# Turning later band groups ahead of their run, inside the feed-forward steps

## The chip, the cores and the metric

The kernel runs on one core of one Trainium2 chip. The metric is device time in microseconds, the median of three runs. A core has five engines that run side by side and wait for each other through semaphores: PE (matrix products; the profile shows its weight loads apart, as PEld), DVE (vector work), ACT (functions of single elements), POOL (a second engine for vector work) and SP, which in this kernel issues nearly all transfers. Products land in eight PSUM banks; everything else is in SBUF or, for inputs, results and two kinds of intermediate data, in DRAM.

## The reference

The input x has shape (2, 256, 128, 128): batch, time, band, channel. Three layers follow, each added to x. Attention over time is causal, with 4 heads of 32; attention over bands is limited to 16 neighbours on either side; the third is a feed-forward layer with 512 hidden channels. Each begins with a normalization over the channels.

```
xt = _ln(x, ln_t_w, ln_t_b).transpose(0, 2, 1, 3)
x = x + _mha(xt, t_wi, t_bi, t_wo, t_bo, H_T, cm).transpose(0, 2, 1, 3)
xf = _ln(x, ln_f_w, ln_f_b)
x = x + _mha(xf, f_wi, f_bi, f_wo, f_bo, H_F, bm)
xn = _ln(x, ln_n_w, ln_n_b)
h = jax.nn.gelu(xn @ w1.T + b1, approximate=False)
x = x + (h @ w2.T + b2)
```

All is float32.

## The kernel before

The work is cut into 384 groups of 512 tokens (128 partitions times NT = 4 columns of 128 channels). The first 128 groups (`OverTime`) do attention over time and write to DRAM. Then come 16 runs. A run holds 8 groups of attention over bands (`OverBands`) and then the same 8 pieces of data as feed-forward groups (`FeedForward`). The input of a band group is read from DRAM; a feed-forward group takes the result of its band group from SBUF.

`BoundedPath.run` (line 1275) goes through the groups in one loop over steps n (line 1313). A step issues pieces of several groups: PE's products for group n, the second part of n - 1, the end of n - 2, and the preparation of later groups. Every instruction goes through `InOrder` (line 897), so each engine, and SP as well, does its work in exactly the order of the calls in the loop; one operation that waits keeps back all behind it on its engine. The profile therefore shows line 907 for nearly everything, and instructions are told apart by their tiles.

How a group is prepared:

- `statistics` (line 390): on DVE, four BATCH_NORM_STATS2 and four BATCH_NORM_AGGREGATE make mean and variance (tiles stats, mv). `root` (line 407): two operations on POOL make rstd, one over the deviation. Band groups get both one run ahead, in the feed-forward step 8 groups earlier (lines 1417 to 1423; those of the first band group come a step later, with the second's).
- `normalize` (line 441): on DVE, four TENSOR_SCALAR, from x to xh (2 buffers).
- `turn` (line 458): one STREAM_TRANSPOSE on DVE from xh to z (2 buffers), then four transfers issued by SP that write z to a DRAM buffer, turned. The pool of these buffers is named turns (line 928).
- `fetch` (line 470): one transfer that reads turned back as xnT, the operand of PE.

Before the change the step in which normalize and turn stand is n + 3 for every band and feed-forward group (line 1384); fetch is issued in the step for n + 2 (line 1376), ahead of it; PE uses xnT of a feed-forward group in step n itself and of a band group one step earlier.

PSUM: in these runs the eight banks go round (`turn_of_bank`, line 943). A feed-forward step takes, in this order, two banks for the first two hidden products (`first_half`, tiles xnT and w1f), one for the output of the group before (`weigh`, tiles hT and w2T_sb, called zp in the code), and two for the other two hidden products (`second_half`). ACT empties the hidden banks with Gelu. DVE empties the output bank in `divide` (line 886), an addition to res; this call stands at line 1406, behind the normalize and turn of the same step. res is then written to the output, with four transfers on SP for every second group.

In a band step DVE has these: `first_function` (line 790), which clamps and masks the scores of the fourth head (bank<-bank,band) ahead of its Exp on ACT; normalize and turn; `finish` (x<-bank,x); three operations of `divide` (line 615); and, in some steps, statistics for feed-forward groups. In the first feed-forward step (called turn in the loop) `invert_exactly` puts one RECIPROCAL in place of two functions on ACT. In the first run, DVE also tests the weights in the third and fourth feed-forward step (`test`, line 1162), and PE sums the tests in the sixth (`verdict`, line 1174).

Of the kernel before, what the change touches and what calls it, by code (L numbers as in the profile page):

```python
# [17 lines left out]
DRAM = bass.MemoryType.DRAM  # L18
# [7 lines left out]
NT = 4  # L26
# [343 lines left out]
class Group:  # L370
# [7 lines left out]
    def __init__(self, path, src, dst, before=None, store=None):  # L378
        self.path, self.src, self.dst = path, src, dst
        self.before, self.store = before, store  # L380
# [531 lines left out]
class BoundedPath:  # L912
    def __init__(self, ctx, tc, k):
        self.tc, self.nc, self.k = tc, tc.nc, k
        self.xpool = ctx.enter_context(tc.tile_pool(name="xpool", bufs=3))
        self.work = ctx.enter_context(tc.tile_pool(name="work", bufs=3))
        self.small = ctx.enter_context(tc.tile_pool(name="small", bufs=6))
        ps = ctx.enter_context(tc.tile_pool(name="ps", bufs=1, space=PSUM))
        self.ps = [ps.tile([P, BANK], F32, name=f"bank{i}", tag=f"bank{i}") for i in range(8)]
        self.next_bank = 0  # L920
        self.inputs = 0
        self.held = {}
        self.banks = dict(zip(("a1", "a2", "b0", "b3", "a0", "a3", "b1", "b2"), range(8)))
        self.tensor, self.vector = InOrder(tc, tc.nc.tensor), InOrder(tc, tc.nc.vector)
        self.scalar, self.gpsimd = InOrder(tc, tc.nc.scalar), InOrder(tc, tc.nc.gpsimd)
        self.sync = InOrder(tc, tc.nc.sync)
        k.wf, k.bq, k.wn, k.orow = [], [], [], []
        self.dram = ctx.enter_context(tc.tile_pool(name="turns", bufs=3, space=DRAM))
        self.zero = 0.0
        self.once = once = ctx.enter_context(tc.tile_pool(name="once", bufs=1))  # L930
        self.tests = once.tile([P, 6], F32, name="tests")
        self.eps = once.tile([P, 1], F32, name="eps")
        tc.nc.vector.memset(self.eps, EPS)

        self.band = once.tile([P, P], F32, name="band")
        tc.nc.gpsimd.memset(self.band, 0.0)
        for s in (1, -1):
            tc.nc.gpsimd.affine_select(
                out=self.band, in_=self.band, compare_op=ALU.is_ge, fill=-1e30, base=BAND,
                pattern=[[-s, P]], channel_multiplier=s,  # L940
            )
# [333 lines left out]
    def run(self, x, out):  # L1275
        groups = list(self.groups(x, out))

        def do(n, *names):
            if 0 <= n < len(groups):
                for name in names:  # L1280
                    getattr(groups[n], name)()

        def at(n, kind):
            return 0 <= n < len(groups) and isinstance(groups[n], kind)

        def do_at(n, kind, *names):
            if at(n, kind):
                do(n, *names)
# [6 lines left out]
        run0 = [i for i in range(len(groups)) if at(i, OverBands)][: RUN // NT]  # L1295
# [6 lines left out]
        def statistics_of_feed(n):  # L1302
            if n + 5 in early:
                do(n + 5, "statistics")
            if at(n + 4, FeedForward) and n + 4 not in early:
                do(n + 4, "statistics", "root")

        groups[-1].last = True

        ff = [i for i in range(len(groups)) if at(i, FeedForward)][2:]  # L1310
# [2 lines left out]
        for n in range(len(groups) + 2):  # L1313
            feeds = [at(n - 2 + i, FeedForward) for i in range(5)]
            bands = [at(n - 2 + i, OverBands) for i in range(5)]
            turn = feeds[2] and bands[1]
# [64 lines left out]
                k.late_weights()  # L1381
            for i in {0: (), 1: (), 2: (14, 15), 3: (16, 17)}.get(n, (n + 14,)):
                do(i, "load")
            do_at(n + 3, (OverBands, FeedForward), "normalize", "turn")
            if n != 1:
                do_at(n + 4, OverTime, "normalize", "turn")
            if old is not None:
# [125 lines left out]
```

## Time and profile before

| | us |
|---|---|
| median of 3 runs | 2633.2 |
| lowest and highest run | 2632.67, 2638.77 |
| span of the profiled execution | 2631.9 |
| time groups, from the start to about | 930 |
| one run of 8 band and 8 feed-forward steps, about | 106 |

The profiled execution gives a span of 2631.9 us, from the first to the last instruction; the granted TensorE clock was 1.000 throughout. The table of stretches cuts the span where the reader asks and sums each engine's busy time in each stretch. The timeline lists instructions in order of start, equal neighbours merged (x4 is four of them), with start, time from the first start to the last end, engine, operation and tiles, and in brackets how long the engine had idled before and what ended that. A tile name stands for all its buffers; bank stands for all eight banks, so that which bank is meant follows from the code.

### The profile page before, as it was taken

To read this page: it belongs to the slowest core of one execution; us is meant where nothing else is said; L and a number is where in the kernel's file an instruction comes from. 1 tells how busy PE (TensorE), PEld (TensorE's weight loads), DVE (VectorE), ACT (ScalarE), POOL (GpSimd) and SP (SyncE) were. 2 spreads that over 40 slices of the span, in tenths; PEclk is the share of its full clock that TensorE was granted. 3 is DMA by queue.
4 is the path that set the end of the run, shared out by engine and by line. 5 is a ranking of instruction groups with operands and counts; after the bars stand their busy time and mean duration, and the time that the engine had idled before them with its cause. 6 is when DMAs were issued, how large, how long until landed. Compare 5 with 4: busy or idle time off the path is not lost.

```text
span 2631.9 us, 156460 instructions
## 1 busy us (share of the span) xinstructions
PE 2617.8 (99%) x68688; PEld 1837.4 (70%) x68688; DVE 2140.8 (81%) x6410; ACT 1838.8 (70%) x3543; POOL 1958.6 (74%) x2311
## 2 busy tenths in 40 slices
PE   9999999999999999999999999999999999999999
PEld 6666666666766767666777776667676677777776
DVE  8888888888888887977878779788797797887974
ACT  7989988999899875564655746647557466475573
POOL 7999999999999987666667666665776666757762
PEclk9999999999999999999999999999999999999999
DMA  6656555565565454445454544554454445554543
GB/s 155 167 149 158 149 149 149 155 155 149 149 158 149 122 127 119 115 123 127 118 124 124 123 122 117 126 128 120 122 126 120 120 119 131 123 120 123 123 104 88
DMA packets 469797, 344.97 MB, mean 131 GB/s; under 512 B 43120, under 2 KB 404464, under 8 KB 469104
## 3 DMA queue, kind: packets, MB, share of 16 engines
q1 hardware_dynamic: 468408, 334.41, 50.5%
q8 instruction: 540, 8.85, 1.5%
q14 instruction: 153, 1.25, 0.2%
q10 hardware_dynamic: 696, 0.46, 0.1%
HBM read 167.98 MB, written 166.72 MB: 127 GB/s over the span
## 4 chain that ended last, share of the span: by engine, by line
PE 99%; DVE 0%; issue 0%; DMA 0%; ACT 0%; ACTq 0%; DVEq 0%
PE bank L907 99%; DMA x<-in_x 0%; DVE xh L907 0%; DVE bank L907 0%; DVE res L907 0%; DVE stats L907 0%; DVE oT L907 0%; DVE u L907 0%; DVE xnT L907 0%; ACTq L907 0%; ACT p L907 0%; DVE vy L907 0%; ACT lnv L907 0%; DVE mv L907 0%; ACT root L907 0%
## 5 line engine op out<-in xcount | busy, mean ns | idle before, releaser
L907 ACT ACTIVATE hT<-bank,b 128x512 f32<-128x512 f32 x512 | 348.1, 688 | 524.2 <-PE bank L907 483.2
L907 POOL TENSOR_SCALAR_AFFINE_SELECT pf<-pf 128x512 f32<-128x512 f32 x768 | 477.7, 637 | 185.3 <-ACT pf L907 159.1
L907 PEld LDWEIGHTS bank<-w2T_sb,hT 128*32 128x32 f32 x16384 | 467.4, 110 | 54.8 <-issue 29.0
L907 PE MATMUL bank<-xnT,wf 128*32 128x512 f32 x4096 | 492.4, 592 | 0.5 <-DVE xnT L907 0.5
L907 PE MATMUL bank<-xnT,w1f 128*32 128x512 f32 x4096 | 486.3, 592 | 0.2 <-issue 0.2
L907 PE MATMUL bank<-w2T_sb,hT 128*32 128x128 f32 x16384 | 482.8, 273 | 1.0 <-issue 1.0
L907 ACT ACTIVATE p<-bank 128x512 f32<-128x512 f32 (+1 forms) x1024 | 430.6, 494 | 62.9 <-PE bank L907 62.9
L907 DVE TENSOR_SCALAR xh<-x,mv,rstd 128x160 f32<-128x160 f32 (+1 forms) x1012 | 394.3, 432 | 59.7 <-POOL rstd L907 49.4
L907 POOL TENSOR_SCALAR_AFFINE_SELECT p<-p 128x1024 f32<-128x1024 f32 (+2 forms) x384 | 364.5, 949 | 57.5 <-ACT p L907 49.1
L907 PEld LDWEIGHTS bank<-wf,xnT 128*32 128x32 f32 x8192 | 243.3, 110 | 144.1 <-issue 101.6
L907 POOL TENSOR_TENSOR p<-p,p 128x512 f32<-128x512 f32 x256 | 324.6, 1291 | 10.6
L907 DVE BATCH_NORM_STATS2 stats<-x 128x6 f32<-128x128 f32 x1536 | 329.0, 276 | 3.4 <-DMA x<-in_x 3.4
L907 POOL TENSOR_SCALAR rstd<-mv 128x4 f32<-128x4 f32 x251 | 57.8, 230 | 361.7 <-DVE mv L907 360.5
L907 PEld LDWEIGHTS bank<-xnT,w1f 128*32 128x32 f32 x4096 | 183.6, 110 | 171.6 <-issue 109.6
L907 PE MATMUL bank<-qT,kT 32*64 32x80 f32 (+4 forms) x16384 | 302.0, 271 | 0.1
L907 PEld LDWEIGHTS bank<-qT,kT 32*64 32x64 f32 x16384 | 260.0, 131 | 51.2 <-ACT kT L907 50.6
L907 DVE TENSOR_TENSOR res<-bank,res 128x512 f32<-128x512 f32 (+1 forms) x259 | 170.3, 658 | 153.3 <-PE bank L907 144.7
L907 ACT ACTIVATE pf<-bank 128x512 f32<-128x512 f32 x512 | 265.8, 602 | 35.5 <-PE bank L907 31.3
L907 PE MATMUL bank<-wn,oT 128*32 128x128 f32 x8192 | 283.8, 274 | 0.1
L907 DVE STREAM_TRANSPOSE z<-xh 128x512 f32<-128x512 f32 x380 | 270.3, 711 | 13.3
L907 PE MATMUL bank<-wf,xnT 128*32 128x128 f32 x8192 | 276.5, 273 | 0.0
L907 POOL TENSOR_TENSOR rstd<-rstd,mhalf 128x4 f32<-128x4 f32 x251 | 260.8, 1039 | 20.9
(100 smaller groups left out, 3820.3 us busy)
## 6 DMA issues: line engine op xcount, KB each, us to landing
turned<-z SPq DMA_DIRECT2D x1520, 64.0 KB, 2.7
xnT<-turned SPq DMA_DIRECT2D x380, 256.0 KB, 3.2
x<-res SPq DMA_DIRECT2D x256, 128.0 KB, 2.5
x<-x SPq DMA_DIRECT2D x128, 256.0 KB, 4.1
out<-res SPq DMA_DIRECT2D x252, 128.0 KB, 2.3
x<-in_x SPq DMA_DIRECT2D x124, 256.0 KB, 4.3
x<-in_x SPq DMA_DIRECT2D x4, 128.0 KB, 2.8
x<-in_x SPq DMA_DIRECT2D x6, 64.0 KB, 2.9
```

The costliest lines, as they stand in the source:

```text
L907: return self.tc.keep_in_program_order(emit(*args, **kwargs))
```

## The change

The call at line 1384 is replaced by a function that looks three and six groups ahead. Three ahead it does what was done before, unless the group has been turned already. Six ahead it normalizes and turns a band group, if that group is not of the first run. All band groups of a later run are so turned in step n + 6: the first three in the third to fifth feed-forward step (before: the sixth to eighth), the 4th to 6th in the sixth to eighth feed-forward step (before: the first three band steps), the 7th and 8th in the first two band steps (before: the fourth and fifth). Feed-forward groups stay at three ahead. By steps of a run this makes one block of normalize and turn more in each of the third, fourth and fifth feed-forward steps, where it stands behind the block of a feed-forward group, and one less in each of the third, fourth and fifth band steps. In all others their number is the same. The pool of DRAM buffers for turned grows from 3 to 8.

```
-        self.dram = ctx.enter_context(tc.tile_pool(name="turns", bufs=3, space=DRAM))
+        self.dram = ctx.enter_context(tc.tile_pool(name="turns", bufs=2 * NT, space=DRAM))
...
+        def turn_ahead(n):
+            for i in (n + 3, n + 6):
+                if at(i, FeedForward) and i == n + 3 or at(i, OverBands) and (i == n + 3 or n > run0[0] and i not in run0):
+                    if not hasattr(groups[i], "turned"):
+                        do(i, "normalize", "turn")
...
-            do_at(n + 3, (OverBands, FeedForward), "normalize", "turn")
+            turn_ahead(n)
```

## The prediction

> **What bounds the kernel now.** Read first the busy shares on the page and the waits of PE in the stretch of the band and feed-forward runs (1040 to 2600 us; the columns of a wait are its total in us, how often, the longest).
>
> ```profile
> PE 2617.8 (99%) x68688; PEld 1837.4 (70%) x68688; DVE 2140.8 (81%) x6410; ACT 1838.8 (70%) x3543; POOL 1958.6 (74%) x2311
> ...
> PE bank L907 <- issue: 2.7, 7, 0.8
> ```
>
> PE is covered for 99% of the span, and of these 1560 us it waited visibly for 2.7, never for DVE. But the page says that matmul ends are modelled, so short stalls can hide under neighbours. Hence the second reading, the table of stretches, one line a step, in the fourteenth run (its feed-forward steps are called f0 to f7, the band steps b0 to b7; the band groups that f2 to f7 prepare are the next run's). Columns: stretch, its length, then PE, PEld, DVE, ACT, POOL busy.
>
> ```profile
> 2339.93:2346.16 6.23, 6.23 (x188) 4.23 (x184) 6.09 (x18) 5.08 (x10) 4.98 (x8) 1.00 0.51 118
> 2368.92:2375.85 6.93, 6.93 (x172) 5.48 (x166) 5.39 (x27) 2.05 (x4) 5.58 (x7) 1.00 0.35 97
> 2375.85:2382.78 6.93, 6.93 (x166) 5.37 (x162) 6.86 (x33) 2.75 (x5) 6.64 (x9) 1.00 0.39 88
> 2382.78:2389.71 6.93, 6.93 (x166) 5.42 (x162) 6.71 (x26) 2.75 (x5) 6.74 (x9) 1.00 0.61 156
> 2389.71:2396.64 6.93, 6.93 (x166) 5.42 (x162) 4.73 (x19) 2.76 (x5) 6.79 (x7) 1.00 0.80 208
> 2396.64:2403.57 6.93, 6.93 (x166) 5.42 (x162) 3.92 (x16) 2.75 (x5) 4.25 (x5) 1.00 0.42 102
> ```
>
> Line 1 is a band step: DVE 6.09 of 6.23 us, full. The others are f2 to f6 by the start of PE's step: DVE is full in f3 and f4 (6.86 and 6.71 of 6.93) and has room only from f5 on (4.73, then 3.92). The change puts its work into f2, f3 and f4. So the question is not how much DVE has on average but how late it already is there, and what waits for it.
>
> **Part 1, band steps: what is removed.** Three normalize-and-turn blocks per run leave steps b2, b3, b4. (Steps b0 and b1 still do one each, for the 7th and 8th group.)
>
> ```profile
> 2327.47 0.70 DVE L907 SCALAR_TENSOR_TENSOR bank<-bank,band 128x512 f32<-128x512 f32 x1 [0.63 <-PE bank L907]
> 2347.12 0.67 DVE L907 SCALAR_TENSOR_TENSOR bank<-bank,band 128x512 f32<-128x512 f32 x1
> 2352.61 0.69 DVE L907 SCALAR_TENSOR_TENSOR bank<-bank,band 128x512 f32<-128x512 f32 x1
> ...
> 2339.66 1.07 PE L907 MATMUL bank<-pf,ones 128*32 128x512 f32 x8
> 2345.89 1.22 PE L907 MATMUL bank<-pf,ones 128*32 128x512 f32 x8
> 2352.28 1.05 PE L907 MATMUL bank<-pf,ones 128*32 128x512 f32 x6
> ```
>
> The clamp of the fourth head came at once in b3 (DVE had idled 0.63). Three steps of 6.23 later it is due at 2346.16 and comes at 2347.12: in b6, DVE has fallen 0.96 us behind (the clamps of b4 and b5 by part of it). The fourth head's Exp and its row of ones-products, a step later, hang on the clamp, and there PE shows it: 2339.66 to 2345.89 is 6.23, the next step 6.39, 0.16 more. Bounds of the gain per run: nothing (the skew lost in the next block) and 0.96 (all the lag). I take what PE shows, 0.16; 15 runs (the first is not touched) make 2.4 us, at most 14.4.
>
> The entry into the feed-forward steps has a second one:
>
> ```profile
> 2367.52 0.43 DVE L907 TENSOR_SCALAR oT<-u 128x512 f32<-128x512 f32 x1
> 2366.16 0.59 PE L907 MATMUL bank<-xnT,w1f 128*32 128x512 f32 x1
> 2368.00 1.14 PE L907 MATMUL bank<-wn,oT 128*32 128x128 f32 x30
> ```
>
> The last band group's output product starts at 2368.00, 0.05 after its operand (2367.95). Two hidden products before it, from 2366.16, take 1.72 (half of the 3.44 of four, below), so it was due at 2367.88: 0.12 waited. Between nothing and 0.12 a run I take the middle, 0.06: 0.9 us in 15.
>
> **Part 2, feed-forward steps: what is added.** One block more in each of f2, f3, f4 (the 1st to 3rd band group of the next run; f5 to f7 have one before and after, of other groups).
>
> ```profile
> 2377.02 1.60 DVE L907 TENSOR_SCALAR xh<-x,mv,rstd 128x160 f32<-128x160 f32 x4
> 2378.66 0.71 DVE L907 STREAM_TRANSPOSE z<-xh 128x512 f32<-128x512 f32 x1
> 2379.30 0.83 DVE L907 BATCH_NORM_STATS2 stats<-x 128x6 f32<-128x128 f32 x4
> 2380.32 0.66 DVE L907 TENSOR_TENSOR res<-bank,res 128x512 f32<-128x512 f32 x1
> 2385.23 0.66 DVE L907 TENSOR_TENSOR res<-bank,res 128x512 f32<-128x512 f32 x1
> 2389.31 0.65 DVE L907 TENSOR_TENSOR res<-bank,res 128x512 f32<-128x512 f32 x1
> 2395.38 0.69 DVE L907 TENSOR_TENSOR res<-bank,res 128x512 f32<-128x512 f32 x1 [2.13 <-PE bank L907]
> ...
> 2381.03 0.60 PE L907 MATMUL bank<-xnT,w1f 128*32 128x512 f32 x2
> 2384.47 3.73 PE L907 MATMUL bank<-w2T_sb,hT 128*32 128x128 f32 x126
> 2387.96 0.60 PE L907 MATMUL bank<-xnT,w1f 128*32 128x512 f32 x2
> 2394.89 0.60 PE L907 MATMUL bank<-xnT,w1f 128*32 128x512 f32 x2
> ```
>
> Price of a block: from 2377.02 to the next operation at 2379.30, 2.28 us, with no idle time near it. In program order the new block stands right behind the old one and ahead of the addition res that empties the previous group's output bank. The four res rows are those of f1, f2, f3, f4. The last one waited for PE, so there DVE has caught up; the first three did not.
>
> Who waits for res? The eight banks go round. A feed-forward step takes five: hidden 0 and 1 of its group, the output of the group before, hidden 2 and 3. Eight turns after f1's output (taken in f2) come: hidden 2 and 3 of f2; hidden 0, 1, output, hidden 2, 3 of f3; hidden 0 of f4. So hidden 0 of f4 must wait until res of f1 has read the bank, and likewise f5 for f2, f6 for f3. A stretch of four hidden products runs 2381.03 to 2384.47, 3.44 us; its second half is hidden 0 and 1 of the next group, so hidden 0 of f4 starts at 2382.75, of f5 at 2389.68, of f6 at 2396.61. The ends of res are 2380.98, 2385.89, 2389.96. Slack today: 1.77, 3.79, 6.65 us. Ahead of them come one, two, three new blocks, 2.28, 4.56, 6.84. **Late by 0.51, 0.77, 0.19**: PE stands 0.51 at f4, another 0.26 at f5, and at f6 the 0.77 already lost is cover enough. DVE does not wait for PE there, so nothing of it comes back: 0.77 us a run, 14 runs, 10.8 us.
>
> In the first run DVE also has the weight tests in f2 and f3 and is later:
>
> ```profile
> 1013.40 0.65 DVE L907 TENSOR_TENSOR res<-bank,res 128x512 f32<-128x512 f32 x1
> 1016.91 0.39 PE L907 MATMUL bank<-tests,ones 128*128 128x6 f32 x2
> ```
>
> This res is f3's; the verdict's product in f5 takes the bank that hidden 0 of f6 takes elsewhere. 14.05 + 6.84 = 1020.89 against 1016.91: 4.0 us once.
>
> The block's inputs hide: its rstd must be there when DVE has done the old block, 2379.30.
>
> ```profile
> 2378.09 1.04 POOL L907 TENSOR_TENSOR rstd<-rstd,mhalf 128x4 f32<-128x4 f32 x1
> ```
>
> It ends at 2379.13, 0.17 ahead. That cover is thin: each 0.1 that POOL is later adds 0.1 to every lateness. The later blocks' rstd were made a step before. Below that, bounds of the added cost: 0 a run, if DVE had a block's room, and 2.28 a run, a whole block. The slack of 1.77 lies nearer to the block than to nothing of it, and gives the 0.5 to 0.8 taken.
>
> Queues: each added block issues four more writes of turned on SP ahead of the step's stores and of the next step's fetch.
>
> ```profile
> 2379.40 2.38 SPq L907 DMA_DIRECT2D turned<-z  x4
> 2381.83 1.99 SPq L907 DMA_DIRECT2D out<-res  x4
> 2383.99 1.21 SPq L907 DMA_DIRECT2D xnT<-turned  x1
> xnT<-turned SPq DMA_DIRECT2D x380, 256.0 KB, 3.2
> ```
>
> Four writes took 1.9 to 2.4 us. In f2 the new four run from 2381.8 to 2383.7, the stores behind them (res at 2383.26) to 2385.7, and the fetch of f5's operand starts at 2385.7 instead of 2383.99. With 3.2 to land it is there at 2388.9, ahead of 2389.68; cost nothing, with 0.8 us of cover (1.3 with the stall). The larger ring of DRAM buffers (3 to 8) costs no instruction; it is needed as up to five turned groups lie between write and fetch. ACT and PE get no instruction more or less.
>
> **Sum.** +10.8 + 4.0 - 2.4 - 0.9 = +11.5 us on the profiled span of 2631.9, which is 1.3 under the median 2633.2 (start and end around the span): 2644.7 us. Own range of this case: 2640 (0.5 us lost and 0.3 gained a run) to 2649 (0.85 lost and nothing gained).
>
> **Rivals.**
>
> A, the delay is absorbed: not slower. PE's slack for the bank is larger than the starts show, or DVE reaches f0 earlier by the 0.96 that it no longer lags and hands that on; it decides once the slack at f4 is 2.28 instead of 1.77. Against: before it reaches f0 the lag is worked off: the clamp of b7 comes at 2352.61, four steps of 6.23 after 2327.47 are 2352.39, so 0.2 can be handed on, of the 0.5 needed. Then only part 1 stays: 2633.2 - 3.3 = 2629.9. The Trainium skill, Perfetto Trace Analysis, section Identifying the Most-Contended Engine, says that matmul busy time does not tell how far PE is from its limit and that the busy share of weight loads does: by that rule PE has 30% to spare (70% above, 5.42 of 6.93 in these steps) and might win 0.8 us back. The trace disagrees: three steps in which DVE is early or late last 6.93 alike, so there is no faster pace to return to.
>
> B, SP is late too. If the fetches for f5 and f7, both behind a step's stores, land after 4.3 us instead of 3.2, as the 256 KB loads of the input do, f5's comes 0.3 us after its time, or hides in the stall; with a slow issue like the 1.21 above it is 1.2. At 0.5 us a run: 2652.
>
> ```profile
> x<-in_x SPq DMA_DIRECT2D x124, 256.0 KB, 4.3
> ```
>
> C, faster: all 0.96 us of DVE's lag was PE's, and the slack suffices. 2633.2 - 14.4 = 2618.8. Against: PE shows 0.16 of it. The Trainium skill, Perfetto Trace Analysis, section Optimization Strategy, holds that where the most loaded engine changes between stages, mixing the stages can pay; this is its case in this kernel. The table speaks against the place: the mixed-in work falls on f3 and f4, which are as full as the band step.
>
> D, nothing: blocks stay where they were, or gain and loss cancel. 2633.2. The condition on the group's index holds from the second run on, so the blocks do move.
>
> **How the numbers follow.** A measurement of this kernel tells about 0.3% from no change, 7.9 us: 2625.3 to 2641.1. Forecast 0.55 (of it 0.06 under 2641.1), A 0.21, B 0.12, C 0.06, D 0.06. Slower: 0.49 + 0.12 = 0.61; within: 0.06 + 0.21 + 0.06 = 0.33; faster: 0.06. The range goes from A, 2629, to 2651, half of B: it leaves out C and half of B, and some of A and of the forecast's edges, under 0.2.
>
> **What would show it.** Right: in the timeline of after, in every run, DVE without idle time from the last band steps to f5; the res of f1 ends after PE's hidden products of f3 are done, and hidden 0 of f4 starts right behind it; steps f4 and f5 last 7.4 and 7.2 us, not 6.93; the band steps are 6.23 throughout. Wrong: f4 and f5 at 6.93 (A); hidden 0 of f5 starting with its fetch's landing rather than with res (B); band steps shorter than 6.23, or feed-forward steps shorter than 6.93 (C). The sum falls most easily by the 0.5 us: a slack wrong by that much is the whole of it.

## The result and the profile after

| | before | after |
|---|---|---|
| median, 6 runs each | 2633.7 us | 2651.3 us |
| lowest and highest run | 2632.67, 2638.77 | 2646.08, 2657.28 |
| span of the profiled execution | 2631.9 us | 2649.7 us |

The changed kernel is slower: its ratio to before is 1.0067, with a 95% interval of 1.0054 to 1.0080, which is 17.6 us at the medians. The forecast was slower by 11.5 us, 2644.7, with an upper end of 2651.0. The sign and the main mechanism came as predicted; the time lies 0.3 us above the range and 6.6 above the forecast: one term that the sum has at zero was not zero.

The page of before has these two lines that the prediction did not show, the shares of the chain that ended last and the group of the first hidden products (busy time and mean; behind the second bar, idle time ahead of them and what ended most of it):

```profile
PE 99%; DVE 0%; issue 0%; DMA 0%; ACT 0%; ACTq 0%; DVEq 0%
L907 PE MATMUL bank<-xnT,w1f 128*32 128x512 f32 x4096 | 486.3, 592 | 0.2 <-issue 0.2
```

The page of after, with the busy shares and the median landing time of the fetches as well:

```profile
PE 2622.6 (99%) x68688; PEld 1766.7 (67%) x68688; DVE 2141.2 (81%) x6410; ACT 1836.0 (69%) x3543; POOL 1957.1 (74%) x2311
...
PE 79%; DVE 16%; DMA 2%; POOL 1%; issue 1%; SPq 1%; ACT 0%; ACTq 0%; DVEq 0%; POOLq 0%
...
L907 PE MATMUL bank<-xnT,w1f 128*32 128x512 f32 x4096 | 478.8, 593 | 15.1 <-DVE res L907 7.0
...
xnT<-turned SPq DMA_DIRECT2D x380, 256.0 KB, 3.4
```

The busy shares say nothing: PE stands at 99% in both. The chain does. It was PE alone, and now a fifth of it is DVE, transfers and SP. The hidden products, which had waited for nothing, wait 15.1 us. What for is in PE's waits from 1040 to 2620 us (total, how often, the longest):

```profile
PE bank L907 <- DVE res L907: 4.6, 13, 0.4
PE bank L907 <- DMA xnT<-turned: 4.6, 5, 1.2
PE bank L907 <- issue: 1.8, 4, 0.5
PE bank L907 <- DVE mv L907: 1.6, 2, 0.9
PE bank L907 <- DVE stats L907: 1.4, 4, 0.5
```

The first is the bank that the prediction named, once in nearly every run. The second, a fetch that has not landed, has no term in its sum. The last two have to be read with care. No hidden product uses mv or stats; a wait for several semaphores is put down to the one that came last, and these too turn out to be fetches, since they stand at f5 and f7 with the bank long free.

The stretches of the fourteenth run, by the start of PE's steps, answer to those of before (b5, then f3 to f6; columns as there):

```profile
2361.15:2367.38 6.23, 6.23 (x190) 4.14 (x184) 6.09 (x17) 5.06 (x9) 4.97 (x8) 1.00 0.50 127
2390.86:2398.32 7.46, 7.11 (x165) 4.43 (x157) 7.32 (x28) 3.12 (x6) 4.90 (x8) 1.00 0.45 102
2398.32:2405.46 7.14, 7.13 (x160) 4.43 (x160) 7.00 (x28) 2.47 (x4) 4.99 (x7) 1.00 0.71 186
2405.46:2412.41 6.95, 6.95 (x160) 4.56 (x164) 6.81 (x26) 2.67 (x4) 6.87 (x7) 1.00 0.44 102
2412.41:2419.66 7.25, 7.11 (x165) 4.44 (x158) 7.11 (x26) 2.91 (x6) 6.96 (x9) 1.00 0.78 182
```

Step f3, from the start of f3 to that of f4, takes 7.46 instead of 6.93, and f4 7.14; both were forecast (7.4 and 7.2, there called steps f4 and f5, after the steps whose start is late). f5 has 6.95. But f6 takes 7.25, which was not forecast. The granted clock is 1.00 throughout, so no step is longer by the clock.

The same spacings for all of the 14 middle runs, summed over what the step takes undisturbed, give this account of the profiled executions (each number is a sum of start-to-start distances of PE's steps):

| place | before | after | forecast of the difference |
|---|---|---|---|
| step f3 (14 runs), 6.93 each | 0.6 | 7.5 | +7.1 |
| step f4, 6.93 each | 0.0 | 6.7 | +3.6 |
| step f6, 6.93 each | 0.0 | 5.4 | 0 |
| the first run's f3 to f6 | 0.6 | 4.6 | +4.0 |
| band steps b1 to b5 (15 runs), 6.23 each | 6.0 | 3.0 | -2.4 |
| entry into the feed-forward steps (15 runs) | 2.1 | 1.2 | -0.9 |

These differences add up to 19.1 us, and the spans differ by 17.8; the rest lies outside the places listed. Step f3 takes 7.45 to 7.54 in every one of the 14 runs. Step f4 takes 7.14 to 7.30 in eight of them and 7.46 to 8.33 in the other six. In f6, seven runs have 6.93 to 6.95 and seven 7.09 to 8.36. So there is a fixed part, the bank, of 6.9 + 14 x 0.22 = 10.0 us, and a part that comes and goes, 3.6 in f4 and 5.4 in f6: 9 us.

The ninth run shows both parts in one step. PE in the timeline:

```profile
1861.70 1.92 PE L907 MATMUL bank<-xnT,w1f 128*32 128x512 f32 x16 [0.34 <-DVE res L907]
...
1870.04 1.92 PE L907 MATMUL bank<-xnT,w1f 128*32 128x512 f32 x16 [1.20 <-DMA xnT<-turned]
```

DVE there, the additions that free the two banks:

```profile
1860.99 0.66 DVE L907 TENSOR_TENSOR res<-bank,res 128x512 f32<-128x512 f32 x1
...
1868.14 0.66 DVE L907 TENSOR_TENSOR res<-bank,res 128x512 f32<-128x512 f32 x1
```

And what SP issues ahead of f5:

```profile
1857.83 5.08 SPq L907 DMA_DIRECT2D turned<-z  x8
1863.01 1.95 SPq L907 DMA_DIRECT2D out<-res  x4
1865.06 0.43 SPq L907 DMA_DIRECT2D xnT<-turned  x1
```

f4 starts 0.05 after the addition for f1 ends (1861.65), as forecast. For f5 the bank is free at 1868.80, but PE starts at 1870.04: its operand was fetched at 1865.06, behind the four stores and eight writes instead of four, and 4.98 us passed until PE could begin, not 3.2. The trace also has the landing of these fetches: those for f5 took 2.95 to 4.85 us from issue to landing in the 14 middle runs, median 3.77, and in seven of these runs PE starts f5 within 0.14 us of the landing (here it came at 1869.90). There the fetch alone ended the wait.

### The profile page after: what moved, and what is told of

It is laid out like the page before. It is cut to its first block, busy times and chain, and to the rows that moved or that the text cites. A ratio compares the mean times of both kernels' runs of the same rounds, so it can differ in the third digit from the quotient of the medians.

```text
span 2649.7 us, 156373 instructions
## 1 busy us (share of the span) xinstructions
PE 2622.6 (99%) x68688; PEld 1766.7 (67%) x68688; DVE 2141.2 (81%) x6410; ACT 1836.0 (69%) x3543; POOL 1957.1 (74%) x2311
## 4 chain that ended last, share of the span: by engine, by line
PE 79%; DVE 16%; DMA 2%; POOL 1%; issue 1%; SPq 1%; ACT 0%; ACTq 0%; DVEq 0%; POOLq 0%
PE bank L907 79%; DVE xh L907 5%; DVE stats L907 3%; DVE z L907 2%; DVE ln L907 1%; DMA xnT<-turned 1%; DVE res L907 1%; DVE mv L907 1%; POOL rstd L907 1%; SPq L907 1%; DVE x L907 1%; DMA turned<-z 1%; DVE bank L907 1%; DVE u L907 0%; DMA x<-x 0%
## 5 line engine op out<-in xcount | busy, mean ns | idle before, releaser
L907 PEld LDWEIGHTS bank<-w2T_sb,hT 128*32 128x32 f32 x16384 | 453.9, 110 | 69.8 <-issue 54.3
L907 PE MATMUL bank<-xnT,w1f 128*32 128x512 f32 x4096 | 478.8, 593 | 15.1 <-DVE res L907 7.0
L907 PE MATMUL bank<-w2T_sb,hT 128*32 128x128 f32 x16384 | 474.5, 273 | 1.6 <-issue 1.3
L907 PEld LDWEIGHTS bank<-xnT,w1f 128*32 128x32 f32 x4096 | 134.1, 110 | 230.5 <-issue 167.1
L907 PE MATMUL bank<-wn,oT 128*32 128x128 f32 x8192 | 276.3, 274 | 0.6 <-issue 0.5
L907 POOL TENSOR_TENSOR rstd<-rstd,mhalf 128x4 f32<-128x4 f32 x251 | 260.6, 1038 | 20.9
L907 DVE TENSOR_TENSOR bank<-bank,r 128x512 f32<-128x512 f32 x240 | 166.9, 695 | 102.1 <-PE bank L907 80.9
```

Of the source, the lines that this page charges most:

```text
L907: return self.tc.keep_in_program_order(emit(*args, **kwargs))
```

## The experiments

The theory from here on: **bank plus fetch**. DVE's late addition costs about 10 us and 4 in the first run, late fetches of f5 and f7 about 9, and the band steps give back 3 to 4. The rival: **one cause**, in which the fetches are late only because the bank wait shifts PE against SP, so that mending the bank mends both; and for the fetches alone, that they were a chance of one execution or only cover some other stall. All times are medians; each ratio is to the kernel before on the same chip.

| experiment | us | before there | ratio, 95% interval |
|---|---|---|---|
| e1_res_first | 2666.2 | 2631.4 | 1.0120 [1.0098, 1.0142] |
| e2_fetch_first | 2647.4 | 2631.4 | 1.0055 [1.0038, 1.0072] |
| e3_both_first | 2651.2 | 2631.4 | 1.0073 [1.0056, 1.0090] |
| e4_last_three | 2630.9 | 2631.4 | 0.9996 [0.9986, 1.0005] |
| e5_split | 2632.3 | 2631.2 | 0.9998 [0.9989, 1.0008] |
| e6_one_f2 | 2641.2 | 2631.2 | 1.0040 [1.0025, 1.0054] |
| e7_one_f3 | 2631.1 | 2631.2 | 0.9999 [0.9989, 1.0008] |
| e8_ring | 2630.9 | 2631.2 | 0.9997 [0.9987, 1.0006] |
| e9_after_again | 2651.3 | 2630.4 | 1.0077 [1.0062, 1.0093] |
| e10_fetch_first_again | 2643.6 | 2630.4 | 1.0045 [1.0032, 1.0058] |
| e11_two_writes | 2644.9 | 2630.4 | 1.0051 [1.0037, 1.0066] |

### One block at a time: e6, e7, e4

Only one of the three blocks stays early. For e6 it is the 1st band group's, in f2; for e7 the 2nd's, in f3:

```
-                if at(i, FeedForward) and i == n + 3 or at(i, OverBands) and (i == n + 3 or n > run0[0] and i not in run0):
+                place = (i - run0[0]) % (2 * RUN // NT)
+                if i == n + 3 and at(i, (FeedForward, OverBands)) or at(i, OverBands) and n > run0[0] and i not in run0 and place == 0:
```

(e7 has place == 1.)

> Only the 1st band group of a later run is turned early, in the third feed-forward step (one block more in f2, one less in f5); all others as before the change. BANK: f3 lasts 7.46 in every run (2.28 against 1.77), f4 has no bank's wait (2.28 against 3.79), only a fetch for f5 that is late at times (up to 1 us); f6 6.93. 7 us of bank, 1 to 5 of fetch, 0.6 in the first run: 2639 to 2645. If DVE's load as such were the cause, f4 and f5 would be longer too.

> Only the 2nd band group of a later run is turned early, in the fourth feed-forward step (one block more in f3, one less in f6): the same work as in the sixth experiment, one step later. BANK: res of f2 is 2.28 late against 3.79, res of f3 against 6.65: no wait, f3 and f4 6.93. The step's stores do not stand between the new writes and the fetch for f6, so no late fetch either. 2631 to 2634, and 0.6 to 1 of it in the first run. DVE LOAD: as slow as the sixth experiment, since f3 is as full as f2's neighbours.

The waits of PE in e6, from 1040 to 2620 us:

```profile
PE bank L907 <- DVE res L907: 2.0, 11, 0.2
PE bank L907 <- DMA xnT<-turned: 1.4, 3, 0.8
```

One block in f2 costs 10.0 us: step f3 is 7.2 us over in 14 runs, 0.52 a run (the prediction had 0.51), and step f4 another 3.6, most of it by late fetches (up to 7.91). The same block in f3 costs nothing: the sums over f3 to f6 are those of before. It fits into the slack of 3.79 at f5, as the single block in f2 does not fit into the 1.77 at f4. That confirms the prediction's slacks, one by one.

e4 leaves the 1st to 3rd group as before and keeps what the change does to the 4th to 8th (two blocks each in f5, f6 and f7):

```
-                if at(i, FeedForward) and i == n + 3 or at(i, OverBands) and (i == n + 3 or n > run0[0] and i not in run0):
+                later = n > run0[0] and i not in run0 and at(i - 3, OverBands)
+                if at(i, FeedForward) and i == n + 3 or at(i, OverBands) and (i == n + 3 or later):
```

> The first three band groups of a run are turned where they were before (sixth to eighth feed-forward step); the 4th to 6th, 7th and 8th as in the changed kernel. So f5, f6, f7 have two blocks each and f2, f3, f4 one; the band steps are those of the changed kernel. DVE has 4.73 and 3.92 of 6.93 us busy there, room for 2.28. BANK+FETCH: no wait for a bank or a fetch, the band's gain alone: 2627 to 2631. Rival THE MOVE ITSELF (turning six ahead costs by its longer way or more live buffers, wherever it stands): 2640 or more.

Its waits of PE:

```profile
PE bank L907 <- issue: 1.8, 6, 0.5
PE bank L907 <- ACT pf L907: 0.2, 1, 0.2
```

Steps f3 to f6 are back at 6.93, but for two of the 14 f3 steps (7.01 and 7.22; before has one of 7.48), and the band step that the prediction had at 6.39 before is 6.23, as in the changed kernel. So the gain in the band steps exists by itself, and the three blocks in f2 to f4 bring the whole loss. In time the gain is not resolved: the interval allows 3.7 us of gain and 1.3 of loss, and the forecast of 3.3 lies in it.

### Which wait is whose: e1, e2, e3, e5

e1 puts the six-ahead block behind the addition res, in every step:

```
-        def turn_ahead(n):
-            for i in (n + 3, n + 6):
+        def turn_ahead(n, ahead):
+            for i in (n + ahead,):
...
-            turn_ahead(n)
+            turn_ahead(n, 3)
...
             do(n - 1, "divide")
+            turn_ahead(n, 6)
```

> The blocks turned six ahead stand behind the addition res of their step instead of ahead of it; nothing else differs from the changed kernel. Theory BANK+FETCH (the loss is 0.53 + 0.22 us a run of waiting for the output bank, 4 in the first run, and some 0.64 us a run of late fetches for the operands of f5 and f7): the bank's part goes, since res of f1, f2, f3 is then late by no, one, two blocks of 2.28 against slacks of 1.77, 3.79, 6.65; steps f3 and f4 return to 6.93 where the fetch is in time; SP has as many writes as before, so 1 to 5 us of late fetches stay. 2634 to 2640 us. Rival FETCH ALONE (the bank's waits hide behind fetches that would be late anyway): 2647 to 2652. Rival DVE LOAD (three blocks in full steps cost PE whatever their order): 2649 to 2653.

A miss by 26 us, and of use. Its waits of PE:

```profile
PE bank L907 <- issue: 9.8, 13, 3.0
PE bank L907 <- ACT kT L907: 7.4, 14, 0.6
PE bank L907 <- DMA xnT<-turned: 5.9, 10, 1.2
```

The wait for res is gone, and step f3 is 6.93 in all 14 runs: the bank is proved. The fetches are still late (step f4 up to 9.11), which is against the rival of one cause: without any bank wait they cost more, not less. And a new wait has come, in band step b1. DVE there:

```profile
2347.82 0.70 DVE L907 TENSOR_TENSOR bank<-bank,r 128x512 f32<-128x512 f32 x1 [2.41 <-ACT r L907]
...
2349.35 0.69 DVE L907 TENSOR_TENSOR oT<-bank,u 128x512 f32<-128x512 f32 x1
2349.95 1.60 DVE L907 TENSOR_SCALAR xh<-x,mv,rstd 128x160 f32<-128x160 f32 x4
2351.59 0.71 DVE L907 STREAM_TRANSPOSE z<-xh 128x512 f32<-128x512 f32 x1
2352.23 0.67 DVE L907 SCALAR_TENSOR_TENSOR bank<-bank,band 128x512 f32<-128x512 f32 x1
2352.80 0.68 DVE L907 TENSOR_TENSOR x<-bank,x 128x512 f32<-128x512 f32 x1
2354.71 0.70 DVE L907 TENSOR_TENSOR bank<-bank,r 128x512 f32<-128x512 f32 x1 [1.23 <-ACT r L907]
```

The same place in the changed kernel:

```profile
2333.33 0.71 DVE L907 STREAM_TRANSPOSE z<-xh 128x512 f32<-128x512 f32 x1
2334.20 0.70 DVE L907 TENSOR_TENSOR bank<-bank,r 128x512 f32<-128x512 f32 x1
...
2335.72 0.69 DVE L907 TENSOR_TENSOR oT<-bank,u 128x512 f32<-128x512 f32 x1
2336.49 0.70 DVE L907 SCALAR_TENSOR_TENSOR bank<-bank,band 128x512 f32<-128x512 f32 x1
```

In the changed kernel the block ends with the transpose that starts at 2333.33, just ahead of the first operation of `divide`, and the clamp follows oT at once (2336.49). In e1 DVE idles 2.41 there, waiting for ACT's reciprocal r, and the block comes behind oT; it stands ahead of the clamp, which comes 2.9 us after oT's start instead of 0.8. ACT's Exp and the next r, which hang on the clamp, come later, and DVE idles another 1.23. So ahead of `divide` the block had filled a wait; behind it, it lengthens the next one. ACT also copies kT late, and PE takes 6.87 or more for b1 in 14 of the 15 later runs (6.23 undisturbed). Steps b2 and b3 are 14.0 us over as well, summed over these runs (1.7 before), in some of them and by up to 3.2 us, mostly without a visible cause; so the loss of e1 is not explained to the end.

e2 sends the stores of a feed-forward group behind the fetch of the next step, so that they no longer stand ahead of it (those of the last three groups stay):

```
-        self.store()
+        if self.last or self.at_once:
+            self.store()
...
             do_at(n + 2, (OverBands, FeedForward), "fetch")
+            if at(n - 2, FeedForward) and not groups[n - 2].at_once:
+                groups[n - 2].store()
```

> The four stores of a feed-forward group are issued behind the next step's fetch instead of ahead of it; DVE's order is that of the changed kernel. BANK+FETCH: the bank's waits stay (f3 7.46, f4 7.15 in every run), the fetches of f5 and f7 leave SP 2 us earlier and are in time, so f4 is never over 7.2 and f6 is 6.93 in every run: 9 us less, 2641 to 2644, and the runs lie closer together than the 2646 to 2657 of the changed kernel. FETCH ALONE: all of the loss goes, 2628 to 2634. DVE LOAD: 2649 to 2653.

In its profile step f3 stays at 7.46, f4 is 7.15 (7.24 in two runs) and f6 6.93, and no fetch is waited for. The total fell less than expected, to 3.4 us over the upper end: in that execution stalls without a visible cause ("issue", up to 1.2 us) in b1 and b2 took part of it. For that reason it was run again, below.

e3 is e1 and e2 together.

> Both reorderings at once. BANK+FETCH: no loss is left but some of the first run's, the band steps' gain of 3 to 6 us stays: 2627 to 2632, faster than before. DVE LOAD: 2649 to 2653. A third cause that neither order touches would leave it over 2635.

That is 19 us over what was expected, and over the 2635 at which the expectation had put a third cause. Step f3 is down to 6.94 and f4 to 6.98 in the mean, but f5 has 5.7 us over in 14 runs: the fetch for f6 now stands on SP behind four stores and eight writes, and goes out 3.4 us ahead of its use in the fourteenth run. b1 has its 6.87 or more again, in all 15 later runs, and b2 and b3 are 5.8 over. The new order moves the shortage to other places.

e5 turns the three blocks at the end of steps f2 to f4 and issues their writes behind the next step's fetch; the 4th to 8th group are as in the change:

```
+            if behind(n + 5):
+                do(n + 5, "send")
...
+            if behind(n + 6):
+                do(n + 6, "normalize", "flip")
```

> The 1st to 3rd band group are still normalized and transposed in the third to fifth feed-forward step, but at that step's end, behind the addition and the statistics, and their four writes of turned are issued in the next step behind its fetch; the other groups as in the changed kernel. BANK+FETCH: res of f1 is not delayed, res of f2 by 2.28 (slack 3.79), of f3 by 4.56 (slack 6.65), and no fetch stands behind a new write that waits for DVE. So f3 to f6 last 6.93 in every later run, the first run loses some 1.4 us of its 4, and the total is that of the kernel with two blocks in each of the last three steps, 2630 to 2633. Rival ORDER DOES NOT HELP (as the first and third experiment might be read, 2666 and 2651): 2645 or more, with late products in f3 to f6.

It is level with before. Steps f3 and f4 are 6.93 in 13 of the 14 runs (once 7.64 and once 7.26); some fetches for f7 are late (3.7 us over all runs). All blocks are still moved and the loss is gone: what cost the time was their place ahead of res and ahead of the fetch, not the work. No version is measurably under before; e4 and e5 only match it.

e8 is before with the ring of eight DRAM buffers and nothing else.

```
-        self.dram = ctx.enter_context(tc.tile_pool(name="turns", bufs=3, space=DRAM))
+        self.dram = ctx.enter_context(tc.tile_pool(name="turns", bufs=2 * NT, space=DRAM))
```

> The kernel before with 8 DRAM buffers for turned instead of 3, nothing else. BANK+FETCH: no difference that can be told, 2631 to 2634. Rival RING (longer way between write and read of a buffer, other addresses, costs in DMA): 2640 or more, with late fetches as in the changed kernel.

It is level, so the ring costs nothing that can be told.

### The size of the fetch: e9, e10, e11

e9 is the changed kernel and e10 is e2 again, timed side by side.

> The changed kernel once more, beside the next one, so that the fetch's part is read from one chip. Theory (the excess is a bank wait of about 10 us and late fetches of about 9 us, less some 4 us of gain): 2646 to 2653, steps f3 to f4 at 7.45 in every later run, f4 to f5 7.15 or more, f6 to f7 over 6.93 in about half of them. Rival (the late fetches of the profiled execution were an accident of it): the same f3 to f4, but f4 to f5 at 7.15 and f6 to f7 at 6.93, and about 2643.

> The changed kernel with the stores of a feed-forward group behind the next step's fetch, once more. Theory (late fetches cost about 9 us): no late fetch, f4 to f5 at 7.15 and f6 to f7 at 6.93, and 4 to 9 us under e9; the earlier run of it was some 4 us under the changed kernel's median, on another chip. Rival (late fetches only hide a stall that then shows elsewhere): within 2 us of e9.

The waits of PE in e10:

```profile
PE bank L909 <- DVE res L909: 4.3, 13, 0.4
PE bank L909 <- issue: 3.1, 6, 1.0
```

And SP around the fetch for f5 in its fourteenth run:

```profile
2392.41 0.34 SPq L909 DMA_DIRECT2D xnT<-turned  x1
2392.80 2.98 SPq L909 DMA_DIRECT2D out<-res  x4
```

The fetch now goes out 0.49 after f4's start (2391.92) and no step waits for it; from issue to use there are 5.4 to 6.8 us at f5 and 4.8 to 6.4 at f7. e10 is 7.7 us under e9, inside the 4 to 9 expected. That is the fetch in total time, and not a sharp figure: the executions of e9 lie between 2644.4 and 2658.1, those of e10 between 2640.6 and 2645.5, and e2, the same order on another chip, was 3.9 under the changed kernel's median. In the profile of e9 the late fetches take 5.2 us (1.9 in f4, 3.3 in f6), against 9 in the first profile. What is left is 13.2 us over before, with an interval of 8.4 to 15.3: the bank and the first run less the gains, for which the forecast had 11.5.

e11 asks whether SP's load alone makes the fetch late, with no block added on DVE: the kernel before with the ring of eight, and with f5 to f7's own turned data written once more to a DRAM buffer that nothing reads. These groups are turned in f2 to f4, so the copies are issued there; where the expectation speaks of the next run's band groups, and of f5 to f7 as the place, it is mistaken.

```
+        if self.twice:
+            spare = path.dram.tile([H, D, NT, P], F32, name="spare")
+            for i in range(NT):
+                path.sync.dma_start(spare[:, :, i, :].rearrange("c a x -> a c x"), z[rows_of(i)])
...
+            groups[i].twice = (i - run0[0]) % (2 * A) in (A + 5, A + 6, A + 7)
```

> The kernel before with eight DRAM buffers and, in f2, f3 and f4 of the runs 0 to 14, a second copy of the writes of the next run's 1st to 3rd band group: SP has the transfers that the change adds there, DVE none of its blocks. Here the copied group is the one that the kernel before turns, so the copies are issued in f5, f6 and f7 of each run, not earlier. Theory (a late fetch needs only four writes more ahead of it on SP): the fetches behind them are issued about 1.9 us later; those with a lead under 5 us are late at times, and 2 to 6 us over the kernel before. Rival (it needs DVE's lag as well): all steps at 6.93, and level with the kernel before, 2631.

The fifth run of e11, PE, DVE and SP in the timeline:

```profile
1435.04 1.92 PE L912 MATMUL bank<-xnT,w1f 128*32 128x512 f32 x16 [0.78 <-DVE stats L912]
```

```profile
1429.48 0.66 DVE L912 TENSOR_TENSOR res<-bank,res 128x512 f32<-128x512 f32 x1
```

```profile
1425.60 3.86 SPq L912 DMA_DIRECT2D spare<-z  x4
1429.56 1.94 SPq L912 DMA_DIRECT2D out<-res  x4
1431.61 0.42 SPq L912 DMA_DIRECT2D xnT<-turned  x1
```

f5 begins at 1435.04, 8.05 after f4. Its bank was free at 1430.14; the fetch went out at 1431.61. The profile names DVE's stats, but what f5 lacked was its fetch: this is the reading used above for mv and stats. Over the 14 runs the fetch for f5 goes out 3.78 us after f4's start (median), against 1.81 in before; step f4 is 8.4 us over and f6 2.5, 10.9 together, and the total is 14.4 us over before, so that about 3.5 stand elsewhere. Four more writes ahead of a fetch are enough, without an added block on DVE, and cost more than the 2 to 6 us expected. The copies shown took 3.86 us for four; in the median such copies follow each other after 0.49. The copy can also hold z longer, so that DVE would wait for that buffer; this was not separated. Step f3 shows 0.52 once, as it does in before (0.55).

## Why the prediction was right, and where it failed

- **Bank wait: right, in place and size.** f4 late by 0.51 forecast, 0.53 measured; f5 by another 0.26, measured 0.22; f6 nothing, measured 0.02. For 14 runs 10.8 forecast, 10.0 measured. e1 removes it by order alone, e6 and e7 confirm the slacks of f4 and f5 separately.
- **First run: right in size, not in place.** 4.0 forecast as one wait at the verdict; measured 4.0, but spread over f3 (0.63), f4 (2.33) and f5 (1.62), with 0.6 there before.
- **Band steps and entry: right in size, partly by luck.** 3.3 forecast; 3.9 in the two profiled executions. What repeats is the step that had 6.39 (1.3 us over in before and 1.9 in e8, which has the same order; under 0.1 in the changed kernel and in e9) and the entry (0.9 less than in before, 1.8 less than in e8). The rest of the 3.9 are stalls that vary: the steps b1 to b5 together are 2.9 over in e8, no more than the changed kernel's 3.0. Rival C, that all of DVE's lag was PE's, is out: none of the steps b1 to b5 is under 6.23.
- **Rival A, DVE hands its earlier time on: out.** DVE waits for rstd at the entry, before and after alike:

```profile
2370.48 1.61 DVE L907 TENSOR_SCALAR xh<-x,mv,rstd 128x160 f32<-128x160 f32 x4 [1.47 <-POOL rstd L907]
```

```profile
2385.51 1.61 DVE L907 TENSOR_SCALAR xh<-x,mv,rstd 128x160 f32<-128x160 f32 x4 [1.47 <-POOL rstd L907]
```

  The first row is of before, 1.56 after f2's start (2368.92); the second of after, 1.58 after it (2383.93). Whatever was gained in the band steps ends there. The prediction's sign of this (DVE without idle time from the last band steps on) was wrong, its conclusion not. The Trainium skill, Perfetto Trace Analysis, section Identifying the Most-Contended Engine, would read PE's headroom from its share of the peak arithmetic and from the busy share of the weight loads. The trace disagrees on the second, as it did before: step f5 of the fourteenth run has 5.42 us of weight loads in 6.93 before and 4.56 in 6.95 after, and none of the steps f2 to f6 is shorter than 6.92. (The prediction's 30% to spare is of the whole page; 5.42 of 6.93 leave 22%.)
- **The failed step: the fetch, "cost nothing, with 0.8 us of cover (1.3 with the stall)".** It cost 7.7 us in total time (e9 against e10) and about 9 in the profiled execution. That is rival B on top of the forecast, which had 2652 and a chance of 0.12; B's sign, hidden 0 of f5 starting with its fetch's landing, came in seven of the 14 runs. Three things were off in the term. First, the issue time came from a single run: the fetch for f5 went out 1.24 after f4's start in the fourteenth run of before, but over 14 runs that is 1.22 to 2.36, with a median of 1.81. After, it goes out 3.90 after the start that f4 would have had (median; 2.95 was reckoned). Secondly, the landing time was the median over the kernel, 3.2, while those for f5 took 2.95 to 4.85, median 3.77, and where PE waited for them 3.1 to 5.0 passed from issue to use, median 4.1. With f5 due 7.70 after that start (6.93 and the 0.77 of the bank), 3.80 are left, so about half the fetches are late. Thirdly, f7 had no term in the sum. Its fetch had 6.8 to 9.9 us between issue and use before, median 7.9, and has 3.0 to 5.2 after, median 3.9: DVE makes f7's z behind two of the added blocks, and on SP the writes of the third, and the stores, stand ahead of the fetch.

The sum with the fetch in it is 11.5 + 7.7 = 19.2 us; measured were 17.6, and 20.9 in e9 (2651.3 against 2630.4).

What stays open: why the landing time spreads so much (whether the stores and writes just issued are ahead of the fetch in the transfer engines was not tried by itself; moving the four stores behind it, which was tried, also moves its issue). The Trainium skill, DMA: Bandwidth & Descriptors, section Queues, rings and completion order, says that each transfer engine takes the descriptors of a ring in their order, though a later one may finish its write first; by that the writes just issued would be ahead of the fetch there too, on the engines that they share. It fits with 3.1 to 5.0 us behind a dozen of them, but no run here separates the two. Open as well are the stalls without a visible cause in the band steps, b1 to b3 above all, which are there before as well, differ from run to run, and are largest in e1.

## What to carry to other kernels

Work moved into a step with room on the average must be checked against two clocks there: when the engine's own queue frees what others wait for, and when the issuing queue gets to the next load behind the added transfers. Take both from all repetitions, and cover a transfer by the long end of its landing times, not by the median. Where an operation is put within a step matters as much as which step: the same block was free in one step, cost over 0.5 us a run in the step before, and behind rather than ahead of a wait for another engine it made a new stall.

## What was not expected of the hardware

- A 256 KB read from DRAM, with a median landing of 3.2 to 3.4 us here, reached PE 3.1 to 5.0 us after its issue in those cases in which PE waited for it at f5 of the changed kernel.
- SP mostly needs about 0.49 us for each of these transfers (1.95 for four stores; one in twenty of the writes takes over 1.4), so four writes more put 1.9 us ahead of everything behind them on SP, and writes that wait for their data hold the others back longer still (5.08 for eight).
